# Layer 2's residual in the third stage: from vector additions to accumulating transfers, and from a written-out order to a table of phases

## The chip, the cores and the metric

The kernel runs on one core of one Trainium2 chip. The metric is the device time of one execution in microseconds (us), as the median of three runs. A core has a matrix engine (TensorE, PE in the profile, with PEld for its weight loads), a vector engine (VectorE, DVE), a scalar engine (ScalarE, ACT), GpSimd (POOL) and SyncE (SP), which here only issues transfers. Each engine takes its own instructions strictly in order and waits for the others through semaphores.

## The reference

A batch of 8192 images of 8 channels, 16 by 16, goes through four residual layers. Each layer adds a convolution-like map of the group-normalised input to that input:

```python
x = x + L0(gn(x))      # a tensor-train product over channel, row and column, plus a bias
x = x + L1(gn(x))      # 3x3 convolution, batch normalisation over the whole batch, relu
x = x + L2(gn(x))      # 3x3 convolution of values quantised to -127..127, plus a bias per channel
x = x + L3(gn(x))      # 3x3 convolution with binarised weights, edge padding, plus a bias per channel
```

`gn` subtracts the mean and divides by the standard deviation over 4 groups of 2 channels. Layer 2's quantisation needs the largest absolute value of the whole normalised batch, and layer 1 needs its batch statistics; so the kernel has three stages, each of which goes through all data once.

## The kernel before

The batch is cut into NT = 64 tiles of 128 images. A tile is a 128 x 2048 float32 array: channel and row on the 128 partitions, image and column on the free axis. The first stage computes layer 0 and layer 1's convolution, the second stage the rest of layer 1 and the maximum for layer 2, the third stage (lines 880 to 1053) layers 2 and 3 of every tile. The change touches the third stage alone.

In the third stage the steps of tile i are functions, one instruction or a few each:

- `rows2` (L907, VectorE, two small instructions), `spread2` (L917, TensorE): layer 2's scale per image, spread over the partitions into PSUM.
- `scale2`, called `v` (L925, VectorE, two instructions of 1024 columns): x times the scale, rounded to 8 bits. `round2`, called `q` (L933, ScalarE): to bfloat16.
- `layer2` (L942, TensorE): the convolution of half a tile, h = 0 or 1, six matmuls into a PSUM tile `pq` of two banks. In the order these are `c2h0` and `c2h1`.
- The residual of layer 2. Half 0: `bias2` (L938, ScalarE) adds the bias to x in place, and `first2`, called `stz` (L951, VectorE), adds the scaled PSUM tile to x. Half 1: `second2`, called `z1` (L955, ScalarE), evacuates the PSUM tile with scale and bias into the scratch `z3[i % 2]`, and `add2`, called `add1` (L958, GpSimd), adds it to x.
- `square3` (`sq`, L962, ScalarE), `sums3` (`sums`, L965, TensorE: 16 matmuls onto 32 columns), `stats3` (`small`, L969, VectorE: five small instructions), `pow3` (L973, GpSimd), `rows3` (L910, VectorE), `spread3` (L920, TensorE): the statistics of layer 3's normalisation.
- `offset3` (`c`, L976, ScalarE), `scale3` (`t`, L982, VectorE, two instructions), `high3` (`hi`, L993, ScalarE, with the edge columns), `low3` (`lo`, L998, GpSimd), `edges3` (`edl`, L1011, ScalarE), `add3` (`corr`, L1003, GpSimd: adds offset and bias to x). For the last three tiles `offset3` does nothing and `add3` runs on VectorE.
- `layer3` (L1014, TensorE): half a tile, 24 matmuls in all for both halves, first those of `hi`, then those of `lo`, into a PSUM tile `pf` of two banks (`c3h0`, `c3h1`). `finish` (`out0`, `out1`, L1025, VectorE) adds it to x, and the second of the two sends the tile out.

The PSUM tiles `pq` and `pf` share one tag, `pc`, with two buffers (L882): they are given out in turn, in the order in which the program asks for them, so each new one waits until the tile two before it has been read.

The order of the stage is a list of (step, tile) pairs. Every engine keeps the order of the list (`InOrder`, L33). The list is `C_HEAD`, written out by hand, then a repeated `TURN` (L1040), then `C_TAIL`, written out by hand. At each `rows2:i` the tile i + 4 is also loaded.

```python
        TURN = [("rows2", 3), ("rows3", -1), ("out1", -3), ("sq", 0), ("c2h0", 1), ("stz", 1), ("spread2", 3), ("spread3", -1),
                ("c", -1), ("c2h1", 1), ("z1", 1), ("add1", 1), ("v", 3), ("sums", 0), ("small", 0), ("pow", 0), ("t", -1),
                ("edl", -2), ("q", 2), ("hi", -1), ("bias", 2), ("lo", -1), ("corr", -1), ("c3h0", -2), ("out0", -2),
                ("c3h1", -2)]
```

Of the kernel before, what the change touches and what calls it, by code (L numbers as in the profile page):

```python
# [8 lines left out]
F32 = mybir.dt.float32  # L9
# [3 lines left out]
AF = mybir.ActivationFunctionType  # L13
ALU = mybir.AluOpType
# [4 lines left out]
P = 128  # L19
C, H, W = 8, 16, 16  # L20
# [5 lines left out]
QS = P // NQ  # L26
BANK = QS * W
# [17 lines left out]

C_HEAD = """
rows2:0 spread2:0 v:0 rows2:1 q:0 spread2:1 c2h1:0 rows2:2 bias:0 v:1 spread2:2 rows2:3 c2h0:0 v:2 z1:0 q:1
spread2:3 stz:0 add1:0 bias:1 c2h1:1 sq:0 c2h0:1 z1:1 v:3 sums:0 stz:1 small:0 q:2 add1:1 c2h0:2 c2h1:2 bias:2  # L50
rows2:4 pow:0 sq:1 rows2:5 rows3:0 z1:2 spread2:4 spread3:0 stz:2 t:0 q:3 sums:1 hi:0 c:0 small:1 v:4 add1:2 pow:1
bias:3 c2h0:3 spread2:5 rows3:1 sq:2 c2h1:3 spread3:1 stz:3 lo:0 sums:2 t:1 rows2:6 corr:0 edl:0 small:2 c:1 q:4
z1:3 hi:1 c3h0:0 pow:2 c3h1:0 v:5 add1:3 rows3:2 out0:0 bias:4 out1:0 lo:1 sq:3 q:5 spread3:2 spread2:6 c2h0:4 c:2
corr:1 edl:1 c2h1:4 rows2:7 z1:4 stz:4 t:2 hi:2 sums:3 c3h1:1 small:3 v:6 c3h0:1 out1:1 c2h1:5 pow:3 bias:5 rows3:3
spread3:3 lo:2 out0:1 q:6 spread2:7 rows2:8 z1:5 edl:2 v:7 c:3 add1:4 sq:4 c2h0:5 c3h0:2 bias:6 t:3 corr:2 stz:5
sums:4 c3h1:2 small:4 add1:5 hi:3 out0:2 c2h0:6 pow:4 rows3:4 sq:5 out1:2 spread2:8 stz:6 spread3:4 t:4 lo:3 c2h1:6
z1:6 corr:3 edl:3 sums:5 c:4 hi:4 small:5 pow:5 bias:7 v:8 q:7 add1:6
""".split()
C_TAIL = """
c2h1:-4 sq:-5 rows2:-2 rows3:-6 out1:-8 spread3:-6 rows2:-1 spread2:-2 c2h0:-4 v:-2 sums:-5 stz:-4 z1:-4 q:-3 t:-6  # L60
edl:-7 c3h0:-7 q:-2 small:-5 c2h1:-3 c:-6 out0:-7 c2h0:-2 hi:-6 add1:-4 sq:-4 pow:-5 rows3:-5 z1:-3 spread3:-5
bias:-2 t:-5 stz:-2 lo:-6 edl:-6 sums:-4 small:-4 bias:-3 corr:-6 c:-5 spread2:-1 c2h0:-3 stz:-3 pow:-4 c3h1:-7
hi:-5 out1:-7 c3h0:-6 rows3:-4 spread3:-4 add1:-3 c2h1:-2 sq:-3 lo:-5 z1:-2 out0:-6 v:-1 c3h1:-6 edl:-5 q:-1 add1:-2
sums:-3 t:-4 corr:-5 c:-4 c3h1:-5 out1:-6 small:-3 sq:-2 pow:-3 hi:-4 out1:-5 lo:-4 rows3:-3 bias:-1 sums:-2 c2h1:-1
small:-2 z1:-1 spread3:-3 edl:-4 c2h0:-1 c3h0:-5 c:-3 t:-3 stz:-1 add1:-1 pow:-2 corr:-3 rows3:-2 c3h1:-4 hi:-3
spread3:-2 sq:-1 out0:-5 c:-2 corr:-4 sums:-1 t:-2 lo:-3 hi:-2 small:-1 pow:-1 out1:-4 c3h0:-4 corr:-2 rows3:-1
out0:-4 edl:-3 c3h0:-3 spread3:-1 t:-1 lo:-2 c3h1:-3 out0:-3 edl:-2 out1:-3 hi:-1 c:-1 lo:-1 c3h0:-2 c3h1:-2 edl:-1
out0:-2 c3h0:-1 out1:-2 corr:-1 c3h1:-1 out0:-1 out1:-1
""".split()

# [6 lines left out]
def tile_net(ctx: ExitStack, tc: tile.TileContext, xb, xt_in, pack0, pack1, pack2, out):  # L79
    nc = tc.nc  # L80
    NT = xt_in.shape[0]

    pe, dve, act, pool = (InOrder(tc, e) for e in (nc.tensor, nc.vector, nc.scalar, nc.gpsimd))
# [78 lines left out]
    L = {}  # L162
# [127 lines left out]
    HALVES = [(0, P // 2), (P // 2, P)]  # L290

    def samples(t):
        return t.rearrange("p (b w) -> p b w", w=W)

    def over_w(stat, a, b):

        return stat[:, a:b].unsqueeze(2).to_broadcast([P, b - a, W])
# [25 lines left out]
    with first as s:  # L323
        small = s.enter_context(tc.tile_pool(name="small1", bufs=3))
# [5 lines left out]
        T = [dict() for _ in range(NT)]  # L330
# [267 lines left out]
        for n in range(NT * NQ):  # L598
            t, q = divmod(n, NQ)
# [62 lines left out]
        t = NT - 1  # L662
# [84 lines left out]
    small = ctx.enter_context(tc.tile_pool(name="small", bufs=4))  # L747
    kept = {}
    with tc.tile_pool(name="p2", bufs=2) as p2, tc.tile_pool(name="ps2", bufs=2, space=PSUM) as ps2:
        T = T2  # L750
# [8 lines left out]
        for k in range(3):  # L759
            nc.tensor.matmul(kps, L["gpad"].rearrange("p q j -> p (q j)"), L["band3"][:, k],  # L760
                             start=(k == 0), stop=(k == 2))
# [83 lines left out]
        for i in range(NT + 4):  # L845
# [4 lines left out]
            elif late:  # L850
                k, j = late.pop(0)
# [12 lines left out]
    inv = const.tile([P, 1], F32, name="inv")  # L864
# [15 lines left out]
    with ExitStack() as s:  # L880
        wk = s.enter_context(tc.tile_pool(name="wk3", bufs=2))
        ps_c = s.enter_context(tc.tile_pool(name="ps_c3", bufs=2, space=PSUM))  # L882
# [4 lines left out]
        T = [dict() for _ in range(NT)]  # L887
# [16 lines left out]
        def halves(t):  # L904
            return t.rearrange("p (h n) -> p h n", h=2)
# [29 lines left out]
            act.copy(q, T[i].pop("v"))  # L935
            T[i]["q"] = q

        def bias2(i):  # L938
            x = halves(T[i]["x"])[:, 0]
            act.activation(x, x, AF.Identity, bias=L["bias2"], scale=1.0)  # L940

        def layer2(i, h):  # L942
            pc = ps_c.tile([P, 2, BANK], F32, name=f"pq_{i}_{h}", tag="pc")
            for k in range(2):
                pv, xv = samples(pc[:, k]), samples(T[i]["q"])[:, (2 * h + k) * QS:(2 * h + k + 1) * QS]
                pe.matmul(pv, L["band2"][:, 1], xv, start=True, stop=False)
                pe.matmul(pv[:, :, 1:W], L["band2"][:, 0], xv[:, :, 0:W - 1], start=False, stop=False)
                pe.matmul(pv[:, :, 0:W - 1], L["band2"][:, 2], xv[:, :, 1:W], start=False, stop=True)
            T[i]["pq", h] = pc.rearrange("p k n -> p (k n)")

        def first2(i):  # L951
            x = halves(T[i]["x"])[:, 0]
            dve.scalar_tensor_tensor(x, T[i].pop(("pq", 0)), inv, x, ALU.mult, ALU.add)

        def second2(i):  # L955
            act.activation(z3[i % 2], T[i].pop(("pq", 1)), AF.Identity, bias=L["bias2"], scale=inv)

        def add2(i):  # L958
            x = halves(T[i]["x"])[:, 1]
            pool.tensor_tensor(x, x, z3[i % 2], ALU.add)  # L960

        def square3(i):  # L962
            act.activation(sq3, T[i]["x"], AF.Square)
# [10 lines left out]
            stats_pow(T[i]["mv"])  # L974

        def offset3(i):  # L976
            if i >= NT - 3:
                return
            T[i]["c"] = small.tile([P, P], F32, name=f"c_{i}", tag="c")
            act.activation(T[i]["c"], o3, AF.Identity, bias=L["bias3"], scale=1.0)  # L980

# [20 lines left out]

        def add3(i):  # L1003
            x = samples(T[i]["x"])
            if i >= NT - 3:
                for a, b in HALVES:
                    dve.scalar_tensor_tensor(x[:, a:b], over_w(o3, a, b), L["bias3"], x[:, a:b], ALU.add, ALU.add)
                return
            pool.tensor_tensor(x, x, over_w(T[i].pop("c"), 0, P), ALU.add)

        def edges3(i):  # L1011
            edges(T[i]["lo"])

        def layer3(i, h):  # L1014
            pc = ps_c.tile([P, 2, BANK], F32, name=f"pf_{i}_{h}", tag="pc")
            for m, t in enumerate(("hi", "lo")):
                for k in range(2):
                    q = 2 * h + k
                    tv = T[i][t][:, q * QS:(q + 1) * QS]
                    for n in range(3):  # L1020
                        pe.matmul(samples(pc[:, k]), L["sign3"][:, n], tv[:, :, n:n + W],
                                  start=(m == n == 0), stop=(m == 1 and n == 2))
            T[i]["pf", h] = pc

        def finish(i, h):  # L1025
            x = halves(T[i]["x"])[:, h]
            pc = T[i].pop(("pf", h)).rearrange("p k n -> p (k n)")
            dve.scalar_tensor_tensor(x, pc, L["scale3"], x, ALU.mult, ALU.add)
            T[i]["done"] = T[i].get("done", 0) + 1
            if T[i]["done"] == 2:  # L1030
                nc.sync.dma_start(out[order[i]], T[i]["x"])
                T[i].clear()

        OPS = {"rows2": rows2, "spread2": spread2, "v": scale2, "q": round2, "bias": bias2,
               "c2h0": lambda i: layer2(i, 0), "stz": first2, "c2h1": lambda i: layer2(i, 1), "z1": second2, "add1": add2,
               "sq": square3, "sums": sums3, "small": stats3, "pow": pow3, "rows3": rows3, "spread3": spread3, "c": offset3,
               "t": scale3, "hi": high3, "lo": low3, "corr": add3, "edl": edges3,
               "c3h0": lambda i: layer3(i, 0), "out0": lambda i: finish(i, 0),
               "c3h1": lambda i: layer3(i, 1), "out1": lambda i: finish(i, 1)}
        TURN = [("rows2", 3), ("rows3", -1), ("out1", -3), ("sq", 0), ("c2h0", 1), ("stz", 1), ("spread2", 3), ("spread3", -1),  # L1040
                ("c", -1), ("c2h1", 1), ("z1", 1), ("add1", 1), ("v", 3), ("sums", 0), ("small", 0), ("pow", 0), ("t", -1),
                ("edl", -2), ("q", 2), ("hi", -1), ("bias", 2), ("lo", -1), ("corr", -1), ("c3h0", -2), ("out0", -2),
                ("c3h1", -2)]
        todo = [(op, i + k) for i in range(-3, NT + 4) for op, k in TURN if 0 <= i + k < NT]
        if len(todo) >= len(C_HEAD) + len(C_TAIL):
            head, tail = ([(op, int(i) + n) for op, i in (c.split(":") for c in l)] for l, n in ((C_HEAD, 0), (C_TAIL, NT)))
            todo = head + todo[len(head):len(todo) - len(tail)] + tail
        for i in range(AHEAD):
            load3(i)
        for op, i in todo:  # L1050
# [72 lines left out]
```

## Time and profile before

| what | value |
|---|---|
| time, median of 3 runs | 3834.26 us (3833.98 to 3834.51) |
| span of the profiled execution | 3831.5 us; what lies around the span in that execution is not given |
| third stage: first `rows2` to the end of the span | 3064.6 to 3831.5 us |
| one tile in the middle of the third stage (start of one `pq` group to the same of the next tile) | 11.55 us |
| ScalarE, one of each: q, z1, bias, sq, c, hi, edges of hi, edl | 1.90, 1.21, 1.15, 1.90, 0.35, 1.93, 0.55, 0.54 us |
| VectorE, one of each: v (both halves), t (both), stz, out | 2.35, 2.34, 1.28, 1.26 us |
| GpSimd, one of each: pow, lo, corr, add1 | 1.02, 4.27, 3.69, 2.42 us |

The page of the profile gives busy time, share of the span and the number of instructions of each engine. A row of windows gives the same for a stretch of time, with the granted clock of TensorE and the busy share of the transfer engines. A timeline line is: start in us from the span's start, length in us, engine, line, operation, what it writes <- what it reads, how many in a row, and in brackets how long the engine stood idle before it and for whom. The line of nearly all instructions is L43, the helper that records them, so they are told apart by their tiles: `pq` layer 2 in PSUM, `pf` layer 3 in PSUM, `s` the sums, `bs` in the third stage mostly the scratch `z3`, `q`, `v`, `sq`, `hi`, `lo`, `mv` as above, `xs`, `u`, `xk`, `ys` (and `bs`) the places where x lies, `sq` and `xh` also the places of `t`.

### The profile page before, as it was taken

To read this page: it belongs to the slowest core of one execution; us is meant where nothing else is said; L and a number is where in the kernel's file an instruction comes from. 1 tells how busy PE (TensorE), PEld (TensorE's weight loads), DVE (VectorE), ACT (ScalarE), POOL (GpSimd) and SP (SyncE) were. 2 spreads that over 40 slices of the span, in tenths; PEclk is the share of its full clock that TensorE was granted. 3 is DMA by queue.
4 is the path that set the end of the run, shared out by engine and by line. 5 is a ranking of instruction groups with operands and counts; after the bars stand their busy time and mean duration, and the time that the engine had idled before them with its cause. 6 is when DMAs were issued, how large, how long until landed. Compare 5 with 4: busy or idle time off the path is not lost. (4 is left out here: it accounts for less than half of the span.)

```text
span 3831.5 us, 52833 instructions
## 1 busy us (share of the span) xinstructions
PE 3606.5 (94%) x16326; PEld 2127.6 (56%) x16326; DVE 3406.9 (89%) x6319; ACT 2513.1 (66%) x2673; POOL 3040.9 (79%) x3101
## 2 busy tenths in 40 slices
PE   8999999999999999999999999997655599999998
PEld 4666666666666666666666666662211155555555
DVE  8988888888888888888888888877998889999997
ACT  5666666666666666666666666665665477777775
POOL 4877778777777787777777877766887779999997
PEclk9999999999999999999999999998776699999999
DMA  5787787888877878788788788757999724444432
GB/s 212 255 268 258 258 266 251 270 253 262 270 256 258 267 250 271 253 262 267 258 261 266 250 271 252 258 187 281 422 425 425 301 110 176 187 185 178 185 145 99
DMA packets 210809, 960.93 MB, mean 251 GB/s; under 512 B 44896, under 2 KB 45152, under 8 KB 110048
## 3 DMA queue, kind: packets, MB, share of 16 engines
q1 hardware_dynamic: 173808, 692.22, 48.7%
q0 software_dynamic: 36288, 264.26, 23.4%
q8 instruction: 131, 2.15, 0.2%
q14 instruction: 150, 1.23, 0.1%
q10 hardware_dynamic: 432, 1.08, 0.1%
HBM read 578.84 MB, written 378.54 MB: 250 GB/s over the span
## 5 line engine op out<-in xcount | busy, mean ns | idle before, releaser
L43 PE MATMUL po<-u,core 128*128 128x512 f32 (+1 forms) x4112 | 1844.7, 591 | 0.0
L43 ACT COPY u<-pu 128x2048 f32<-128x2048 f32 x512 | 956.7, 1868 | 511.9 <-PE pu L43 511.8
L43 PEld LDWEIGHTS po<-u,core 128*128 128x128 f32 x4112 | 744.7, 190 | 737.1 <-issue 736.1
L43 PE MATMUL pu<-core2r,xl 128*128 128x256 f32 x4032 | 678.5, 310 | 4.5 <-ACT u L43 3.6
L43 PEld LDWEIGHTS pu<-core2r,xl 128*128 128x128 f32 x4032 | 527.9, 189 | 127.8 <-issue 123.0
L43 POOL TENSOR_TENSOR bs<-bs,xh 128x512 fp32r<-128x512 f32 (+1 forms) x253 | 325.6, 1287 | 201.0 <-ACT xh L43 200.9
L43 POOL TENSOR_TENSOR v<-e 128x128 f32<-128x128 f32 x750 | 397.9, 542 | 0.0
L43 DVE TENSOR_TENSOR xs<-po,xs 128x512 f32<-128x512 f32 x256 | 177.0, 692 | 217.5 <-PE po L43 217.5
L43 ACT ACTIVATE m<-pm,b 128x128 f32<-128x128 f32 x250 | 92.0, 368 | 395.5 <-PE pm L43 395.5
L43 PEld LDWEIGHTS pm<-v,fast 128*128 128x128 f32 x2000 | 262.5, 191 | 119.7 <-issue 106.2
L43 POOL TENSOR_TENSOR e<-x1n,x 128x512 f32<-128x512 f32 x250 | 306.2, 1225 | 23.9 <-ACT x L43 16.4
L43 DVE TENSOR_TENSOR bs<-bs,stat 128x1024 f32<-128x1024 f32 x252 | 290.8, 1217 | 2.1
L43 POOL TENSOR_TENSOR xs<-xs,w 128x2048 f32<-128x2048 f32 x64 | 291.5, 4554 | 0.6 <-DMA xs<-in_xt 0.6
L43 PE MATMUL pm<-v,fast 128*128 128x128 f32 x2000 | 263.6, 275 | 0.0
L43 ACT ACTIVATE x<-x1n 128x512 f32<-128x512 f32 x500 | 247.1, 545 | 7.6 <-DVE x1n L43 7.6
L43 POOL TENSOR_TENSOR mv<-mv,mhalf 128x4 f32<-128x4 f32 x127 | 130.8, 1030 | 138.1 <-DVE mv L43 138.1
L43 PE MATMUL pf<-hi,sign 128*128 128x512 f32 x768 | 227.7, 434 | 0.5 <-DVE xs L43 0.5
L43 POOL DMA_DIRECT2D xl<-limb_d x252 | 150.0, 595 | 96.9 <-ACT x L43 29.1
L43 PE MATMUL pf<-lo,sign 128*128 128x512 f32 x768 | 219.4, 423 | 0.0
L43 POOL TENSOR_TENSOR v<-r 128x128 f32<-128x128 f32 x500 | 215.9, 448 | 0.0
L43 ACT ACTIVATE sq<-xs 128x2048 f32<-128x2048 f32 x103 | 196.8, 1911 | 4.7 <-POOL xs L43 4.6
L43 PE MATMUL gb<-rows_c,sel 128*128 128x128 f32 x128 | 40.3, 409 | 167.3 <-DVE rows_c L43 167.3
(310 smaller groups left out, 7202.4 us busy)
## 6 DMA issues: line engine op xcount, KB each, us to landing
xl<-limb_d POOLq DMA_DIRECT2D x252, 1024.0 KB, 7.4
x_d<-xs SPq DMA_DIRECT2D x76, 1024.0 KB, 8.4
xs<-in_xt SPq DMA_DIRECT2D x64, 1024.0 KB, 7.5
bs<-in_xb SPq DMA_DIRECT2D x63, 1024.0 KB, 5.7
limb_d<-xh SPq DMA_DIRECT2D x1008, 64.0 KB, 4.3
limb_d<-bs SPq DMA_DIRECT2D x1008, 64.0 KB, 5.2
y_d<-ys SPq DMA_DIRECT2D x60, 1024.0 KB, 8.0
u<-x_d SPq DMA_DIRECT2D x34, 1024.0 KB, 5.9
```

The source lines that it names most:

```text
L43: return self.tc.keep_in_program_order(op(*args, **kwargs))
```

## The change

Layer 2's residual: both halves are now evacuated by ScalarE with scale and bias into a scratch of their own (`z0`, `z1`), and each is added to x by a transfer from SBUF to SBUF with addition, which GpSimd issues (`acc0`, `acc1`). `bias`, `stz` and `add1` go. The three last tiles are no longer an exception in `offset3` and `add3`. `layer3` is split into its `hi` part (a) and its `lo` part (b), so that other steps can stand between them. The lists `C_HEAD`, `TURN` and `C_TAIL` go: each step has a phase, and the list is sorted by 11.25 times the tile's number plus the phase.

```diff
-C_HEAD = """
...
-C_TAIL = """
...
+PERIOD = 11.25
+PHASE = {"rows2": 0, "spread2": 0.01, "v": 0.1, "q": 1.2, "c2h1": 8.1, "z1": 11.1, "acc1": 13, "c2h0": 14.9, "z0": 19.7,
+         "acc0": 19.8, "sq": 25.4, "sums": 33.8, "small": 33.81, "pow": 33.9, "rows3": 33.91, "spread3": 39.7, "c": 42.4,
+         "t": 45, "hi": 45.2, "lo": 51.1, "edl": 54.2, "corr": 55.9, "c3h1a": 56.3, "c3h1b": 56.31, "c3h0a": 56.4,
+         "out1": 56.41, "c3h0b": 56.42, "out0": 56.43}
...
-        def bias2(i):
-            x = halves(T[i]["x"])[:, 0]
-            act.activation(x, x, AF.Identity, bias=L["bias2"], scale=1.0)
...
-        def first2(i):
-            x = halves(T[i]["x"])[:, 0]
-            dve.scalar_tensor_tensor(x, T[i].pop(("pq", 0)), inv, x, ALU.mult, ALU.add)
-
-        def second2(i):
-            act.activation(z3[i % 2], T[i].pop(("pq", 1)), AF.Identity, bias=L["bias2"], scale=inv)
-
-        def add2(i):
-            x = halves(T[i]["x"])[:, 1]
-            pool.tensor_tensor(x, x, z3[i % 2], ALU.add)
+        def evacuate2(i, h):
+            act.activation(z3[h], T[i].pop(("pq", h)), AF.Identity, bias=L["bias2"], scale=inv)
+
+        def add2(i, h):
+            x = halves(T[i]["x"])[:, h]
+            pool.dma_start(x, z3[h], accum_op=ALU.add)
...
         def offset3(i):
-            if i >= NT - 3:
-                return
...
         def add3(i):
             x = samples(T[i]["x"])
-            if i >= NT - 3:
-                for a, b in HALVES:
-                    dve.scalar_tensor_tensor(x[:, a:b], over_w(o3, a, b), L["bias3"], x[:, a:b], ALU.add, ALU.add)
-                return
             pool.tensor_tensor(x, x, over_w(T[i].pop("c"), 0, P), ALU.add)
...
-        def layer3(i, h):
-            pc = ps_c.tile([P, 2, BANK], F32, name=f"pf_{i}_{h}", tag="pc")
-            for m, t in enumerate(("hi", "lo")):
-                for k in range(2):
-                    q = 2 * h + k
-                    tv = T[i][t][:, q * QS:(q + 1) * QS]
-                    for n in range(3):
-                        pe.matmul(samples(pc[:, k]), L["sign3"][:, n], tv[:, :, n:n + W],
-                                  start=(m == n == 0), stop=(m == 1 and n == 2))
-            T[i]["pf", h] = pc
+        def layer3(i, h, m):
+            if m == 0:
+                T[i]["pf", h] = ps_c.tile([P, 2, BANK], F32, name=f"pf_{i}_{h}", tag="pc")
+            pc, t = T[i]["pf", h], T[i]["hi" if m == 0 else "lo"]
+            for k in range(2):
+                q = 2 * h + k
+                tv = t[:, q * QS:(q + 1) * QS]
+                for n in range(3):
+                    pe.matmul(samples(pc[:, k]), L["sign3"][:, n], tv[:, :, n:n + W],
+                              start=(m == n == 0), stop=(m == 1 and n == 2))
...
-        TURN = [("rows2", 3), ("rows3", -1), ("out1", -3), ("sq", 0), ("c2h0", 1), ("stz", 1), ("spread2", 3), ("spread3", -1),
...
-            todo = head + todo[len(head):len(todo) - len(tail)] + tail
+               "c3h0a": lambda i: layer3(i, 0, 0), "c3h0b": lambda i: layer3(i, 0, 1), "out0": lambda i: finish(i, 0),
+               "c3h1a": lambda i: layer3(i, 1, 0), "c3h1b": lambda i: layer3(i, 1, 1), "out1": lambda i: finish(i, 1)}
+        todo = [(op, i) for _, op, i in sorted((PERIOD * i + at, op, i) for op, at in PHASE.items() for i in range(NT))]
```

Sorted, the middle of the stage repeats one cycle for each tile. With n the tile whose layer 3 is computed, each engine gets, in this order:

- TensorE: spread2:n+5, c3h1a:n, sums:n+2, c3h1b:n, c3h0a:n, c3h0b:n, c2h0:n+4, spread3:n+2, c2h1:n+5
- VectorE: rows2:n+5, t:n+1, small:n+2, v:n+5, out1:n, rows3:n+2, out0:n
- ScalarE: hi:n+1 (before it), q:n+5, sq:n+3, z0:n+4, c:n+2, edl:n+1, z1:n+5, then hi:n+2
- GpSimd: pow:n+2, acc1:n+4, lo:n+1, acc0:n+4, corr:n+1, then pow:n+3

More of the change, by code (lines that the diff above doesn't have):

```diff
@@ L44, in __getattr__ @@
         return call
-C_HEAD = """
[L49 to L58, printed above, removed]
-C_TAIL = """
-c2h1:-4 sq:-5 rows2:-2 rows3:-6 out1:-8 spread3:-6 rows2:-1 spread2:-2 c2h0:-4 v:-2 sums:-5 stz:-4 z1:-4 q:-3 t:-6
@@ L61 @@
[L61 to L69, printed above, removed]
+PERIOD = 11.25
[3 more added lines that the diff above has]
+         "out1": 56.41, "c3h0b": 56.42, "out0": 56.43}
@@ L1032, in finish @@
                 T[i].clear()
-        OPS = {"rows2": rows2, "spread2": spread2, "v": scale2, "q": round2, "bias": bias2,
-               "c2h0": lambda i: layer2(i, 0), "stz": first2, "c2h1": lambda i: layer2(i, 1), "z1": second2, "add1": add2,
+        OPS = {"rows2": rows2, "spread2": spread2, "v": scale2, "q": round2,
+               "c2h0": lambda i: layer2(i, 0), "z0": lambda i: evacuate2(i, 0), "acc0": lambda i: add2(i, 0),
+               "c2h1": lambda i: layer2(i, 1), "z1": lambda i: evacuate2(i, 1), "acc1": lambda i: add2(i, 1),
                "sq": square3, "sums": sums3, "small": stats3, "pow": pow3, "rows3": rows3, "spread3": spread3, "c": offset3,
                "t": scale3, "hi": high3, "lo": low3, "corr": add3, "edl": edges3,
-               "c3h0": lambda i: layer3(i, 0), "out0": lambda i: finish(i, 0),
-               "c3h1": lambda i: layer3(i, 1), "out1": lambda i: finish(i, 1)}
-        TURN = [("rows2", 3), ("rows3", -1), ("out1", -3), ("sq", 0), ("c2h0", 1), ("stz", 1), ("spread2", 3), ("spread3", -1),
[L1041 to L1046, printed above, removed]
-            todo = head + todo[len(head):len(todo) - len(tail)] + tail
+               "c3h0a": lambda i: layer3(i, 0, 0), "c3h0b": lambda i: layer3(i, 0, 1), "out0": lambda i: finish(i, 0),
+               "c3h1a": lambda i: layer3(i, 1, 0), "c3h1b": lambda i: layer3(i, 1, 1), "out1": lambda i: finish(i, 1)}
+        todo = [(op, i) for _, op, i in sorted((PERIOD * i + at, op, i) for op, at in PHASE.items() for i in range(NT))]
         for i in range(AHEAD):
```

## The prediction

> **What bounds the kernel now.** I read, in this order: the page's busy shares, the chain of work that ended last, the windows of the third stage, then the timelines of one tile.
>
> ```profile
> 3696.67 1.85 PE s L43 x16
> 3698.53 6.42 PE pf L43 x24
> 3704.95 1.31 PE pq L43 x6
> ```
>
> The chain runs through TensorE from 3132 to 3751 us, in pieces like these: nothing else ends last. The windows agree (after the stretch: busy us and instructions of PE, PEld, DVE, ACT, POOL; granted clock, transfer share, GB/s):
>
> ```profile
> 3300.00:3400.00 100.00, 100.00 (x509) 57.94 (x508) 93.15 (x167) 79.40 (x72) 97.58 (x35) 1.00 0.47 180
> ```
>
> TensorE is never idle, GpSimd nearly never. A busy TensorE need not be at its peak, so I take its starts:
>
> ```profile
> 3312.20 1.47 PE L43 MATMUL pq<-q,band 128*128 128x512 bf16 x6
> 3313.51 0.39 PE L43 MATMUL ps_a<-rows_d,sel 128*128 128x128 f32 x2
> ...
> 3314.18 1.46 PE L43 MATMUL pq<-q,band 128*128 128x512 bf16 x6
> 3315.57 1.06 PE L43 MATMUL s<-xs,wsum 128*32 128x512 f32 x8
> ...
> 3317.42 1.82 PE L43 MATMUL pf<-hi,sign 128*128 128x512 f32 x6
> 3319.08 1.71 PE L43 MATMUL pf<-lo,sign 128*128 128x512 f32 x6
> 3320.63 1.73 PE L43 MATMUL pf<-hi,sign 128*128 128x512 f32 x6
> 3322.19 1.71 PE L43 MATMUL pf<-lo,sign 128*128 128x512 f32 x6
> 3323.74 1.47 PE L43 MATMUL pq<-q,band 128*128 128x512 bf16 x6
> ```
>
> From start to start: pq 1.31, three spreads 0.67, pq 1.39 ahead of s, s 1.85, pf 1.66 behind s, then 1.55, 1.56, 1.55. That is 11.54 us a tile, the same to 0.01 us in every tile, and a group has these lengths wherever it stands (a pf group ahead of s takes 1.64, at 3781 us). So it is the cost of the matmuls and not of a wait: **no order of the same matmuls makes a tile shorter than 11.5 us**. The other engines:
>
> ```profile
> 3306.01 0.69 DVE L43 TENSOR_REDUCE s_d<-s 128x32 f32<-128x512 f32 x1 [0.23 <-PE s L43]
> ...
> 3307.47 2.34 DVE L43 TENSOR_TENSOR xh<-xs,ps_r 128x1024 f32<-128x1024 f32 x2
> 3308.24 2.42 POOL L43 TENSOR_TENSOR xs<-xs,bs 128x1024 f32<-128x1024 f32 x1
> 3309.73 1.28 DVE L43 SCALAR_TENSOR_TENSOR bs<-pf,scale,bs 128x1024 f32<-128x1024 f32 x1
> 3309.85 1.93 ACT L43 CAST hi<-xh 128x2048 fp32r<-128x2048 f32 x1 [2.28 <-DVE xh L43]
> ...
> 3313.31 1.89 ACT L43 ACTIVATE sq<-xs 128x2048 f32<-128x2048 f32 x1
> ...
> 3315.11 0.34 ACT L43 ACTIVATE c<-ps_o,bias 128x128 f32<-128x128 f32 x1
> 3315.67 1.21 ACT L43 ACTIVATE bs<-pq,bias,inv 128x1024 f32<-128x1024 f32 x1 [0.22 <-PE pq L43]
> ```
>
> They give the latencies used below: s_d starts 0.14 after the group behind s (3305.87); small is 1.46 (to 3307.47); ScalarE starts 0.04 after VectorE's end (3309.81); an engine's next instruction starts about 0.1 before the last one's end (sq 1.89, next at 1.80).
>
> [...] at the stage's start six pq matmuls take 2.51 us (3070.48), later 1.31. [...] No accumulating transfer is in this trace. [...] lo takes 4.27 us beside whatever VectorE runs.
>
> **The change, part by part.**
>
> Removed: bias (64 x 1.15 us of ScalarE), stz (64 x 1.28 of VectorE), add1 (64 x 2.42 = 155 of GpSimd). TensorE's 11.54 covered all three, so by themselves they are worth nothing.
>
> Added: z0, 64 x 1.21 on ScalarE, and two transfers a tile. *Issue on GpSimd*: the nearest row is the limb fetch, 595 ns[...]; I take 0.7. GpSimd then has 1.02 + 4.27 + 3.69 + 1.4 = 10.4 us a tile, with gaps 10.6. *Landing*: [...] 7.4 us (the limb fetch, 1 MB beside a 0.8 busy transfer side); I take 5. Share of the transfer engines: 0.47 x 11.55 = 5.4 us a tile for 2 MB now; 1 MB of accumulation adds 2.7[...], no bound. Neither bound can be a gain, since TensorE waits for neither now.
>
> Moved: everything, by the table. Call S the moment at which sums:n+2 ends on TensorE. From S the table gives TensorE c3h1b:n, c3h0a, c3h0b, c2h0:n+4, spread3, c2h1:n+5, spread2, c3h1a:n+1, sums:n+3. Its groups, with the lengths above: 1.66 + 1.56 + 1.55 + 1.31 + 0.45 + 1.31 + 0.22 + 1.64 + 1.85 = 11.55, no gain. But VectorE now has **v:n+5 behind small:n+2**, ScalarE has q:n+5, sq:n+3, z0:n+4 in a row, and the two PSUM buffers alternate, so c3h1a:n+1 takes the one that z0:n+4 has to empty. That closes a ring of one tile:
>
> S, 0.14, small 1.46, v 2.34, 0.04, q 1.80, sq 1.80, z0 1.21, 0.10 to TensorE (0.05 from q to pq at 3070.48; VectorE's 0.15 at most), c3h1a 1.64, sums 1.85 = **12.38 us**.
>
> A second ring goes S, 0.14, small 1.46, v 2.26, out1 1.19, rows3 0.79, out0 1.26, 0.15, c2h1 1.31, spread2 0.22, c3h1a 1.64, sums 1.85 = 12.27 (c2h1 takes out0's buffer, c2h0 out1's). Both exceed TensorE's 11.55, so the period is 12.38: 0.83 us a tile. TensorE stands 0.5 us ahead of c2h0, 0.2 ahead of c2h1, 0.1 ahead of c3h1a[...].
>
> Waits beside the ring: acc0:n+4 waits on GpSimd for z0's end (S + 8.8); behind it are corr:n+1 (to S + 13.2) and pow:n+3, whose input comes at S + 14.0; covered as long as an issue takes under 1.5 us. lo:n+1 ends at S + 7.7, before edl on ScalarE (S + 9.0). sq:n+3 starts at S + 5.8 and its transfer was issued at S - 3.5: 9.3 us for a landing of 5. Loads and stores on SP keep their places at rows2 and out; a load's slot was sent out four tiles before.
>
> The head, from rows2:0 (3064.6) as 0: v:0 to 3.8, q:0 5.8. c2h1:0 stands ahead of spread2:1 and runs at half clock, to 8.4; v:1 to 11.3, q:1 13.2, c2h1:1 15.4, v:2 18.2, q:2 20.1, c2h1:2 22.0, sums:0 24.2, small:0 25.8. From here the ring binds, without c3: v:3 28.1, q:3 30.1, sq:1 31.9, sums:1 33.8, small:1 35.4, v:4 37.8, q:4 39.7, sq:2 41.5, z0:3 42.6, c3h1a:0 44.4, sums:2 **46.2**. Landings up to 6.5 us hide behind q.
>
> 59 periods follow, while there are tiles for v: 59 x 12.38 = 730.4.
>
> The tail, from the end of sums:61, at 11.55 or less: sums:62 10.0, sums:63 18.7, c3 of 61 23.5, spread3:63 23.9, c3h1a:62 25.5; lo:62 follows pow:63 on GpSimd, so c3h1b:62 starts at 26.3, c3 of 62 ends at 31.0. Now that corr is on GpSimd to the end, corr:62 (3.7) stands ahead of lo:63, to 33.7; edl 34.3, c3 of 63 39.0, out0 40.4, and 5.0 for the last store as now (its issue follows 3826.4): **45.4**.
>
> Sum: 46.2 + 730.4 + 45.4 = 822.0 against 3831.5 - 3064.6 = 766.9: +55.1 (59 x 0.83 = 49, head and tail 6). The profiled execution's span becomes 3886.6; the runs' median lies 2.8 above the span, which I keep: **3889 us**.
>
> **The rivals.** *TensorE stays dense* (the other side): if c3h1a does not wait for z0, nor c2h1 for out0, because buffers go to whichever tile frees one first, both rings are open and the period is 11.55: 46.2 + 681.5 + 45.4 = 773.1, +6, 3840 us: no change, or with a shorter head a small gain. It decides once the rings fall below 11.55. For it: the alternation is read in the code, not seen. Against it: with two buffers the next to come free is z0's anyway.
> *Late landings*: at over 9.3 us from issue to landing sq waits for acc0 and the period grows by the excess; at 10.5 us 13.6, +71, 3960 us. For it: 19.6 us landings under a full transfer side in the second stage. Against it: this stage uses 0.47.
> *GpSimd as the bound*: 9.2 + 2 issues exceeds 12.38 from 1.6 us an issue; at 2.0 13.2, +48, 3938 us.
>
> **How the numbers follow.** Chances: forecast 0.72, dense 0.06, a gain at head and tail on top of that 0.02, late landings 0.12, GpSimd 0.08. The forecast's own range is 3889 +- 16 (0.15 us of latencies x 59 = 9, head and tail 7). To hold 8 in 10 the range takes in GpSimd's case and the first of the late landings: 3868 to 3942. A measurement of this kernel can tell about 0.2% (8 us) from no change. Faster 0.02, same 0.06, slower 0.92.
>
> **What would show it.** Right: starts of s_d 12.4 us apart; TensorE's share near 93% in the stage, its idle time ended by VectorE (ahead of pq) and ScalarE's bs (ahead of pf); ScalarE idle about 3 us ahead of each q for v; no wait for a transfer ahead of sq. Wrong: s_d 11.55 apart (dense), sq waiting for a transfer, or pow waiting behind an issue of 1.6 us and more.

## The result, and the profile after

The changed kernel takes 3898.74 us (3897.29 to 3900.11), the kernel before beside it 3834.12: a ratio of 1.0171, interval 1.0159 to 1.0184. It is **slower by 64.6 us**; 3889 was forecast, 3868 to 3942 the range. The profiled execution has 3898.44 us and a span of 3896.7, so 1.7 us lie around the span.

The windows of the stage (after the stretch: busy us and instructions of PE, PEld, DVE, ACT, POOL; granted clock, transfer share, GB/s):

```profile
3400.00:3500.00 100.00, 96.96 (x459) 55.38 (x465) 74.98 (x144) 72.20 (x66) 87.09 (x41) 1.00 0.89 254
```

Every engine's busy share fell against the row shown of before, and 459 matmuls stand in 100 us where 509 stood in that row (from 3300 to 3700 us, 1841 for 2016): no engine is full any more. The transfer engines went from 0.47 to 0.89.

The timeline of one cycle of the changed kernel, which is where the prediction's rings can be read off:

```profile
3402.55 0.69 DVE L43 TENSOR_REDUCE s_d<-s 128x32 f32<-128x512 f32 x1 [2.82 <-PE s L43]
3404.01 2.35 DVE L43 TENSOR_TENSOR v<-xk,ps_a 128x1024 int8<-128x1024 f32 x2
3405.61 1.72 PE L43 MATMUL pf<-lo,sign 128*128 128x512 f32 x6
3406.39 1.90 ACT L43 CAST q<-v 128x2048 bf16<-128x2048 int8 x1 [3.44 <-DVE v L43]
3407.61 1.46 PE L43 MATMUL pq<-q,band 128*128 128x512 bf16 x5 [0.28 <-DVE u L43]
3408.20 1.91 ACT L43 ACTIVATE sq<-u 128x2048 f32<-128x2048 f32 x1
3409.56 1.47 PE L43 MATMUL pq<-q,band 128*128 128x512 bf16 x6
3410.01 1.19 ACT L43 ACTIVATE bs<-pq,bias,inv 128x1024 f32<-128x1024 f32 x1
3410.86 0.39 PE L43 MATMUL ps_a<-rows_d,sel 128*128 128x128 f32 x2
3411.25 1.81 PE L43 MATMUL pf<-hi,sign 128*128 128x512 f32 x6
3412.99 1.06 PE L43 MATMUL s<-u,wsum 128*32 128x512 f32 x8
3414.98 0.69 DVE L43 TENSOR_REDUCE s_d<-s 128x32 f32<-128x512 f32 x1 [2.82 <-PE s L43]
```

From s_d to s_d 12.43 us, the same to 0.03 in all 59 cycles. A ring is a chain of waits that comes back to the same step one tile later, so the sum of its pieces is the period. Follow it here: s_d to v 1.46, v to q 2.38, q to sq 1.81, sq to z0 (the first `bs`) 1.81, z0 to c3h1a 1.24, c3h1a to s 1.74, s to s_d 1.99: 12.43. TensorE's own loss is 0.44 us ahead of c2h0 (start to start 2.00, where 1.56 is the group's length), 0.22 ahead of c2h1 (ps_o starts at 3409.12, and 0.22 is its length) and 0.25 ahead of c3h1a (0.39 behind ps_a, where 0.14 is enough): 0.91, and 12.43 - 0.91 = 11.52 us of matmuls. sq starts straight behind q: no transfer holds it up.

The longest wait of the stage in the changed kernel (us in total, times, longest; 3300 to 3700 us) is ScalarE's ahead of q, the 3.4 us of the timeline, once a tile:

```profile
ACT q L43 <- DVE v L43: 110.3, 32, 3.5
```

The account of the span, 65.2 us more: 59 cycles of 12.434 us in place of 11.546 make 52.4; the rest, 12.8, is head and tail.

### The profile page after: what moved, and what is told of

The parts are those of the page before. It is cut to its first block, busy times and chain, and to the rows that moved or that the text cites. A ratio compares the mean times of both kernels' runs of the same rounds, so it can differ in the third digit from the quotient of the medians.

```text
span 3896.7 us, 52947 instructions
## 1 busy us (share of the span) xinstructions
PE 3644.1 (94%) x16264; PEld 2137.3 (55%) x16326; DVE 3312.4 (85%) x6249; ACT 2510.6 (64%) x2676; POOL 3021.3 (78%) x3168
## 3 DMA queue, kind: packets, MB, share of 16 engines
q14 instruction: 152, 1.24, 0.1%
## 4 chain that ended last, share of the span: by engine, by line
PE 75%; DVE 17%; issue 3%; DMA 3%; POOL 1%; ACT 1%; POOLq 0%; DVEq 0%; SPq 0%; ACTq 0%
PE po L43 44%; PE pu L43 12%; PE pm L43 6%; PE pf L43 3%; PE s L43 3%; DVE top L43 3%; PE pc L43 3%; DVE v L43 3%; PE pq L43 3%; DVE xs L43 2%; DVE u L43 2%; DVE s_d L43 1%; DVE ys L43 1%; DVE xk L43 1%; PE gb L43 1%
## 5 line engine op out<-in xcount | busy, mean ns | idle before, releaser
L43 POOL TENSOR_TENSOR e<-x1n,x 128x512 f32<-128x512 f32 x250 | 306.2, 1225 | 21.8 <-ACT x L43 14.3
L43 ACT CAST q<-v 128x2048 bf16<-128x2048 int8 x64 | 121.5, 1899 | 230.8 <-DVE v L43 214.2
L43 PE MATMUL pq<-q,band 128*128 128x480 bf16 (+1 forms) x706 | 190.7, 391 | 31.6 <-ACT q L43 9.1
```

Source lines behind the costliest of these rows:

```text
L43: return self.tc.keep_in_program_order(op(*args, **kwargs))
```

## The experiments

**Theory**: small ahead of v on VectorE ties each tile's start to the last one's sums; two rings of nearly equal length follow, through ScalarE (q, sq, z0) and through VectorE (out1, rows3, out0). **Rivals**: the new residual is itself the cost (landing of the transfers, GpSimd's issues, ScalarE's second evacuation); or the order on ScalarE alone.

### v ahead of small

```diff
-PHASE = {"rows2": 0, "spread2": 0.01, "v": 0.1,
+PHASE = {"rows2": 0, "spread2": 0.01, "v": 0.03,
```

> One phase of the changed kernel is altered: v gets 0.03 in place of 0.1, so VectorE runs v:n+5 ahead of small:n+2 and no longer behind it. Ring theory: this takes small out of the way of v, q, sq, z0 and c3h1a, and v out of the way of out1, rows3, out0 and c2h1 (that ring falls from 12.27 to about 10.0 us), so TensorE is dense again: starts of s_d 11.55 to 11.65 us apart in place of 12.43, 59 x 0.85 = 50 us less, about 3845 us (3838 to 3855). Theory that the transfers bind (their engines are 0.89 busy at 12.43 us a tile, 11.1 us of work): the spacing stays at 12.2 or more, 3885 us or more, with sq waiting for acc0. Theory that GpSimd binds: the spacing stays as well, with GpSimd never idle.

Measured: 3845.02 us, ratio to the kernel before 1.0030 (1.0019 to 1.0041). s_d is 11.53 us apart. The window of this kernel:

```profile
3400.00:3500.00 100.00, 99.58 (x496) 58.36 (x503) 82.48 (x158) 80.17 (x69) 92.93 (x45) 1.00 0.96 273
```

496 matmuls, with the accumulating transfers in place and the transfer engines at 0.96. One swap of two neighbours on one engine gives back 53.7 of the 64.6 us (52.3, if each kernel is set against the kernel before that was timed beside it): small ahead of v was the cost, and the rest is head and tail. The transfer engines now stand close behind TensorE: 0.96 of 11.53 us is 11.1 us a tile.

### Without the transfers

Layer 2's result is not added to x in this kernel; everything else is as in the kernel after.

```diff
-"acc1": 13, ... "acc0": 19.8, 
```

> The changed kernel without its accumulating transfers: both halves are still evacuated, but layer 2's result is not added to x, so that part of the computation is left out. Ring theory: no transfer is in the ring, the spacing of s_d stays at 12.4 us; the head is about 4 us shorter, because GpSimd's first addition[...] no longer stands behind two issues: 3894 us (3888 to 3898). Theory that the transfers or their issues are the cause: the spacing falls towards 11.55, about 3845 us.

Measured: 3894.61 us, ratio 1.0163 (1.0146 to 1.0180), s_d 12.43 apart. The same wait, in this kernel:

```profile
ACT q L43 <- DVE v L43: 110.3, 32, 3.5
```

Unchanged: the transfers lie in no ring of this order. Most of the 4.1 us by which this kernel is faster is in the head: the third s_d comes at 3112.72 us for 3116.63. What the transfers take can be read by difference: the transfer engines fall from 0.89 to 0.44, and from pow's start to lo's end GpSimd takes 5.27 us in place of 6.21 (with one issue between), so an issue costs it 0.94 us, 0.65 ahead of lo and 0.28 by which lo's record is longer.

### sq ahead of q

```diff
-"sq": 25.4,
+"sq": 23.5,
```

> The kernel after with sq:n+3 ahead of q:n+5 on ScalarE (its phase 23.5 in place of 25.4), in the time in which ScalarE is idle ahead of q. Theory (two rings of nearly the same length, each closed by small being ahead of v on VectorE): the ring through q, sq and z0 loses sq's 1.8 us and falls to about 10.6, but the ring through out1, rows3, out0, c2h1 and c3h1a is untouched and binds at 12.3 us, so almost nothing is won: s_d 12.3 us apart, some 7 us in all, about 3891 us (3885 to 3898). Rival (the order q, sq, z0 on ScalarE alone is the cost, and VectorE's part in the second ring is covered): 1.8 us less a tile, to TensorE's 11.55, about 3847 us. Second rival (sq now stands ahead of its accumulating transfer's landing, issued 3.5 us before the end of the sums): sq waits for the transfer, q behind it starts later, 3900 us or more.

Measured: 3883.68 us, ratio 1.0133 (1.0120 to 1.0147): 15 us less, where 7 were expected, and just outside the expected 3885 to 3898. s_d is 12.17 apart. The timeline shows the second ring alone:

```profile
3408.24 0.69 DVE L43 TENSOR_REDUCE s_d<-s 128x32 f32<-128x512 f32 x1 [2.57 <-PE s L43]
3409.70 2.35 DVE L43 TENSOR_TENSOR v<-ys,ps_a 128x1024 int8<-128x1024 f32 x2
3410.48 1.92 ACT L43 ACTIVATE sq<-xk 128x2048 f32<-128x2048 f32 x1 [2.27 <-DMA xk<-bs]
3411.97 1.28 DVE L43 SCALAR_TENSOR_TENSOR u<-pf,scale,u 128x1024 f32<-128x1024 f32 x1
3413.95 1.24 DVE L43 SCALAR_TENSOR_TENSOR u<-pf,scale,u 128x1024 f32<-128x1024 f32 x1
3415.25 1.47 PE L43 MATMUL pq<-q,band 128*128 128x512 bf16 x6
3416.70 1.79 PE L43 MATMUL pf<-hi,sign 128*128 128x512 f32 x6
3420.41 0.69 DVE L43 TENSOR_REDUCE s_d<-s 128x32 f32<-128x512 f32 x1 [2.56 <-PE s L43]
```

1.46 to v, 2.27 to out1, 1.98 to out0, 1.30 to c2h1, 1.31 to spread2 (3416.56), 0.14 to c3h1a, 1.72 to s (3418.42), 1.99 to s_d: 12.17. So taking 1.8 us out of the one ring wins 0.26, because the second was right behind it; TensorE's 11.52 stay out of reach as long as small is ahead of v. The rival that put the cost on ScalarE's order alone (3847) falls. sq now does wait for its transfer, up to 3.4 us, but in time in which ScalarE was idle anyway.

### The order of before with the new residual

```diff
+        new = {"bias": [], "stz": ["z0", "acc0"], "add1": ["acc1"]}
+        todo = [(o, i) for op, i in todo for o in new.get(op, [op])]
```

> The kernel before, its order kept (written-out head and tail, repeated turn, VectorE's addition for the last three tiles), with layer 2's residual done as in the change: bias drops out, stz becomes z0 and acc0, add1 becomes acc1. Ring theory: the order is the cause, so TensorE stays dense at 11.55 us a tile and the time is near that of before, 3825 to 3845 us; GpSimd has room, but acc1 now stands behind corr and lands late for sq, so a few tenths a tile may be lost. Theory that the transfers are the cause: 12.2 us a tile or more, 3880 us or more.

Measured: 3994.16 us, ratio 1.0424 (1.0407 to 1.0442): **the theory that the order alone is the cause missed**, by some 150 us. The time lies where the other one, that the transfers are the cause, had put it (3880 us or more); for this order it is right. ScalarE and GpSimd in its timeline:

```profile
3407.11 1.91 ACT L43 ACTIVATE sq<-xs 128x2048 f32<-128x2048 f32 x1 [4.26 <-DMA xs<-bs]
3408.93 1.19 ACT L43 ACTIVATE bs<-pq,bias,inv 128x1024 f32<-128x1024 f32 x1
3410.27 1.20 ACT L43 ACTIVATE bs<-pq,bias,inv 128x1024 f32<-128x1024 f32 x1
...
3411.77 0.88 POOL L43 DMA_DIRECT2D u<-bs  x1 [0.44 <-ACT bs L43]
...
3420.31 1.91 ACT L43 ACTIVATE sq<-u 128x2048 f32<-128x2048 f32 x1 [3.76 <-PE pq L43]
```

In that list sq:n stands ahead of z0:n+1 and z1:n+1, and acc1 follows z1. That is a ring through the landing: sq to z0 1.82, to z1 1.34, to the issue 1.50, to the next sq 8.54: 13.20 us, the distance of the two sq. I had looked for rings through the engines and had not carried the landing round. This kernel has no fixed period: between head and end of the stage two sq are 10.5 to 23.1 us apart, 13.9 on average, so 13.2 is what the ring took in this cycle. From 3300 to 3700 us sq waits for a transfer in 27 of 29 tiles. Why the distances vary so much stays open. The wait ahead of the second sq is put down to TensorE's pq, which sq neither reads nor writes, so I took the transfer to have ended it as it did a cycle earlier; the next experiment takes the transfers out.

### The order of before, new residual, no transfers

Layer 2's result is not added here either.

```diff
-        new = {"bias": [], "stz": ["z0", "acc0"], "add1": ["acc1"]}
+        new = {"bias": [], "stz": ["z0"], "add1": []}
```

> The order of the kernel before with both halves of layer 2 evacuated by ScalarE and the accumulating transfers left out (layer 2's result is not added). It tells what made the old order with the new residual 13.2 us a tile. Theory (a ring through the landing: sq:n, z0:n+1, c, z1:n+1, issue of acc1:n+1, landing 8.5 us, sq:n+1; 1.8 + 1.1 + 0.25 + 1.2 + 0.3 + 8.5 = 13.2): without transfers the ring is open and TensorE's 11.55 us return, 3836 us (3830 to 3846). Rival (the second evacuation on ScalarE, between sq and z1, is the cost by itself): the period stays above 12.5 us, 3900 us or more.

Measured: 3832.19 us, ratio 0.9997 (0.9989 to 1.0006), s_d 11.55 apart. The transfers were the whole 162 us (their issues went with them; by the waits of sq, it was the landing), and the second evacuation on ScalarE costs nothing here. It says more: with the addition gone altogether, the kernel is no faster than before. In this order, in which TensorE fills the stage with its matmuls, no form of the residual can be worth anything.

### The table's order with the old residual, twice

The steps bias, stz, z1 and add1 are those of the kernel before again: first with bias ahead of c2h0 in the list (phase 14.8), then with bias at phase 11.3, which is earlier and not one period later, as the expectation has it: straight behind z1, ahead of hi, q and sq:

```diff
-"z0": 19.7, "acc0": 19.8, "acc1": 13,
+"add1": 13, "bias": 14.8, "stz": 19.7,
```

```diff
-"bias": 14.8,
+"bias": 11.3,
```

> The changed kernel with its table of phases and the split of layer 3, but with layer 2's residual as before: bias on ScalarE (phase 14.8), stz on VectorE at z0's phase, add1 on GpSimd at acc1's phase, no transfers between SBUF and SBUF. Ring theory: v, behind small, still holds up out1, rows3, out0 and with it c2h1; the ring through z0 is gone, but that through out0 stays: 12.27 us a tile, so 59 x 0.15 = 9 us less than the changed kernel, and 4 us less at the head [...]: 3885 us (3875 to 3895). Theory that the transfers are the cause: 11.55 us a tile, about 3840 us.

> The order of the table with the residual of the kernel before (bias, stz, add1), as in the experiment of the old residual, but with bias one period later, behind z1 and ahead of hi on ScalarE (phase 11.3 in place of 14.8), where ScalarE is idle. Theory (there, bias behind q and sq held up stz, which held up rows2, spread2 and c3h1a): stz now follows out0 at once on VectorE, and the ring is 0.14, small 1.46, v 2.26, out1 1.19, rows3 0.8, out0 1.2, stz 1.2, rows2 0.5, 0.25, spread2 0.25, c3h1a 1.73, sums 1.85 = 12.8 us a tile: about 3920 us (3900 to 3935). Rival (bias is not what made stz late): above 4000 us. Second rival (once bias is out of the way the old residual has the same ring as the new one): 12.2 us, 3885 us.

Measured: 4053.0 us, ratio 1.0575 (1.0559 to 1.0591), s_d 14.3 or 15.9 us apart, 14.9 on average, where both theories had less than 3900 us; then 3903.13 us, 1.0181 (1.0166 to 1.0197). The timeline of the first shows why it missed:

```profile
3414.50 1.91 ACT L43 ACTIVATE sq<-xs 128x2048 f32<-128x2048 f32 x1
3416.32 1.13 ACT L43 ACTIVATE u<-u,bias 128x1024 f32<-128x1024 f32 x1
...
3417.48 1.28 DVE L43 SCALAR_TENSOR_TENSOR u<-pq,inv,u 128x1024 f32<-128x1024 f32 x1 [1.67 <-ACT u L43]
...
3419.24 0.49 PE L43 MATMUL ps_a<-rows_d,sel 128*128 128x128 f32 x2 [1.91 <-DVE rows_d L43]
```

bias stood behind q and sq, stz waited for bias, rows2 stands behind stz on VectorE, and spread2 with c3h1a and the sums behind rows2: one more ring, with a wait that my edit had added. Out of the way (11.3), the period is 12.57, with stz (1.2) in the second ring; the sum gave 12.8, and the time lies within the expected 3900 to 3935. So in the table's order the new residual's ring (12.43) is 0.14 us a tile shorter than the old one's: the residual is not what makes this order slow.

### GpSimd's pause in the head

The head of the changed kernel took 52.0 us (3064.5 to the end of sums:2), 46.2 were predicted. GpSimd's timeline there, kernel after:

```profile
3063.24 0.38 POOL L851 PARTITION_ALL_REDUCE gm<-pm  x1 [8.51 <-DVE pm L850]
...
3087.84 0.85 POOL L43 DMA_DIRECT2D xk<-bs  x1 [5.58 <-ACT bs L43]
3095.73 1.05 POOL L43 TENSOR_TENSOR mv<-mv,mhalf 128x4 f32<-128x4 f32 x1 [7.04 <-issue]
```

pow:0 starts 7.0 us behind an issue and waits for nothing that is shown; its input was there at 3091.5. The trace has two MODIFY_POOL_CONFIG instructions right behind that issue (3088.5), and in the kernel before, where an addition comes next on GpSimd, right behind the all-reduce (3063.7). So I took the 7.0 us to come with the first arithmetic instruction behind the all-reduce, and not with the issues. Edit, with a result that nothing uses (the expectations further down call it "the early library"):

```diff
     nc.gpsimd.partition_all_reduce(gm, pm, P, bass_isa.ReduceOp.max)
+    pool.tensor_tensor(pm, pm, mhalf[:, 0:1], ALU.mult)
```

> The kernel after with one small GpSimd multiplication right behind the all-reduce ahead of the third stage (its result is used by nothing). Theory (in the head pow:0 starts 4.2 us late [...]): [...] pow:0 starts right behind mv at about 3091.5, and the head is 4.2 us shorter: 3894.5 us (3893 to 3897), the period 12.43 as before. Rival (the 7 us ahead of pow:0 are the cost of the four issues that stand in front of it[...]): pow:0 stays where it is, 3898.7 us.

Measured: 3895.34 us, ratio 1.0164 (1.0150 to 1.0178). That interval overlaps that of the kernel after, so the reading rests on the trace of this kernel:

```profile
3070.68 0.18 POOL L43 TENSOR_TENSOR pm<-pm,mhalf 128x1 f32<-128x1 f32 x1 [7.02 <-issue]
...
3092.00 1.06 POOL L43 TENSOR_TENSOR mv<-mv,mhalf 128x4 f32<-128x4 f32 x1 [2.69 <-DVE mv L43]
```

The 7 us moved to where nobody waits, pow:0 now waits for VectorE alone, and the third s_d comes 3.3 us earlier (3113.35 for 3116.63), the period as before. The rival (the issues themselves) falls.

### Order edits together, and confined

```diff
+    pool.tensor_tensor(pm, pm, mhalf[:, 0:1], ALU.mult)
-PHASE = {"rows2": 0, "spread2": 0.01, "v": 0.1,
+PHASE = {"rows2": -3.2, "spread2": -3.19, "v": 0.03,
...
+            if i >= NT - 3: (offset3 and add3 as in the kernel before)
```

> The kernel after with four edits of the order around its residual: v ahead of small (the ring opened, 11.52 us a tile), the early library, rows2 and spread2 of a tile ahead of c2h1 of the tile before it (phases -3.2 and -3.19), and corr of the last three tiles on VectorE again. Theory: 3845.0 of the kernel with v first, less 4.2 for the library, 2.5 for the two waits for lo at the end, and about 3 for spread2:1 ahead of c2h1:0 in the head: 3835 us (3832 to 3841), no faster than the kernel before, since TensorE's 11.5 us a tile set the stage in both. Rival (the new residual or its order costs something else that the ring had covered): above 3843 us. Second rival (the new residual is worth something once TensorE is dense): below 3828 us.

Measured: 3855.79 us, ratio 1.0059 (1.0047 to 1.0072): a miss by 21, and worse than v ahead of small alone. The head was 6.8 us shorter (third s_d at 3107.99 for 3114.79), but the period rose to 11.83: spread2, now ahead of c2h1, waits in every tile for rows2. On TensorE ps_o starts at 3409.96, spread2 at 3410.39 and c2h1 at 3410.72: 0.43 and 0.33, where 0.22 each is the length. The 0.31 us by which the period is above 11.52 make 18 us in 59 tiles, and the end was 2.0 longer (30.8 us from the last s on, for 28.8), which I put down to corr on VectorE ahead of t. Then each edit only where it helps:

```diff
+        def early(op, i, at):
+            if i < 4 and op in ("rows2", "spread2"):
+                return at - 3.2
+            return 56.35 if i >= NT - 2 and op == "corr" else at
```

(corr of the last two tiles on VectorE; v at 0.03 and the added multiplication kept)

> The kernel after with v ahead of small, the early library, rows2 and spread2 moved ahead (by 3.2) for the first four tiles alone, and corr on VectorE, behind t, for the last two tiles alone. Theory: the combined kernel's head was 6.8 us shorter than that of the kernel with v first (end of sums:2 at 3108.0 and 3114.8), but its spread2 waited for rows2 in every tile, 0.31 us each, and corr on VectorE ahead of t made its end 1.9 us longer; with both confined the sum is 3845.0 - 6.8 - 1.4 (the wait for lo of the last tile) = 3837 us (3833 to 3841), period 11.53. Rival (the head is won only because tiles further on start early, and is given back behind it): 3843 to 3846 us.

Measured: 3835.03 us, ratio 1.0006 (0.9998 to 1.0014), period 11.53: the time of the kernel before, with the new residual in place. The end is 27.9 us from the last s on. The window of this kernel:

```profile
3400.00:3500.00 100.00, 99.53 (x500) 58.01 (x507) 83.06 (x152) 78.34 (x70) 93.65 (x43) 1.00 0.96 272
```

So with the transfers in place nothing of the loss is left: it was order and place, and not the cost of the new addition. No version that does the whole computation beat the kernel before.

## Why the prediction was right

**Floor and period.** TensorE's 11.55 us as the floor: 11.52 as the sum of the groups in the changed kernel, 11.53 measured in two orders (v ahead of small, edits confined). "The same in every tile" holds for the kernel before in its middle, some 53 tiles; nearer the ends its s_d are 5 to 18 us apart. Ring through ScalarE 12.38: 12.43 measured, every term within 0.1. Second ring 12.27: 12.17, with 0.11 less from out0 to c2h1, 0.08 less for spread2 ahead of c3h1a (0.14 for 0.22) and 0.08 more from c3h1a to s. Stalls 0.5, 0.2 and 0.1 ahead of c2h0, c2h1, c3h1a: 0.44, 0.22, 0.25. The 59 periods: 730.4 predicted, 733.6 measured. That the mechanism is this one is shown by v ahead of small, which opens both rings.

**The head, the term that was mis-sized most**: 46.2 against 52.0. The end of sums:0 was 1 us late, and 4.7 came between sums:0 and sums:1. I had looked at what bias, stz and add1 cost and found them free; what add1 did beside its work, being GpSimd's first arithmetic behind the all-reduce, was not on my list (in the kernel before add1:0 waits 10.84 us for bs there, and pow:0 has no pause ahead of it). The added multiplication gives back 3.3 us; what is left, some 2.5, I did not take apart (the granted clock is 0.73 over the head, 0.50 from 3064 to 3075 us as in the kernel before, and six groups of pq there take 1.96 to 2.77 us, where I counted one so and a record at granted clock 1.00 is 1.47).

**The tail**: 45.4 against 46.6. TensorE waits for lo in each of the last two tiles: c3h1b starts 3.22 and 3.15 us behind c3h1a, where 1.64 and 1.55 are enough, so 1.6 us each. The prediction's times hold 0.8 and 1.8. The first is the one that was too short: pow:63 stands behind corr:61 for some 0.6 us, and lo's record there is 4.67 us and not 4.27.

**Around the span**: 2.8 us taken, 1.7 measured. This 1.1 us goes the other way from the errors of head (5.8), periods (3.2) and tail (1.2).

**What surrounds the ring.** *Issue*: 0.7 taken, my estimate above the 595 ns of the limb fetch, 0.94 measured, below the 1.5 at which corr would have held up pow; GpSimd takes 10.8 us a tile (87.1% of 12.43) for my 10.4. *Landing*: 5 taken, my estimate below the 7.4 of the limb fetch with its 1 MB, 5.0 the median, against a slack of 9.3. *Transfer engines*: 0.89 x 12.43 = 11.1 us a tile, of which the accumulation is 0.45 x 12.43 = 5.6 for 1 MB, and the plain 2 MB 5.5. So a byte of the accumulation took twice the time of a plain one. From 3300 to 3700 us the accumulations move 33.76 MB in 9264 packets and the plain transfers 67.51 MB in 9280: their packets are half as long as well, so a price per packet would show the same, and no run separates the two.

**The rivals.** *Dense*: wrong, the buffers do alternate (c3h1a starts 0.05 us behind z0's end, at 3411.20). *Late landings*: not in this order, but that kind of ring, at 13.9 us on average, is what the old order has with the new residual; my 9.3 us of slack came from the table, not from the transfer. *GpSimd as the bound*: no.

**The signs.** s_d 12.4 apart, ScalarE idle 3.4 ahead of q, idle time of TensorE ended by VectorE ahead of pq and by bs ahead of pf, no transfer ahead of sq: all seen. TensorE's share in the window was a bad sign: 97% for my 93%, although it does lose 0.91 of 12.43 us. A group's record goes on beyond the start of the next (pq 1.46 us long, 1.30 apart; the ends of matmuls are modelled in this profile), so the share hides short stalls; starts and the count of matmuls (1841 for 2016 in 400 us) show them.

## What to carry to other kernels

An order in which each engine looks dense can still close a ring from one tile to the next: write the steps of one cycle in a row, from the end of one reduction to the next, and compare the sum with the bound engine's floor; where two rings are close, mending one wins only their difference. Ask of every asynchronous step how far its landing is from its next use in that very order: the same transfers cost 4 us in one order and 162 us in another. And when an instruction is removed, look at what it started besides its own work.

## What the runs showed of the hardware

- An accumulating transfer of 512 KB from SBUF to SBUF took 0.94 us of GpSimd and a median of 5.0 us to landing at a transfer share of 0.89 (medians of 7.0 to 8.1, by the place of x, in the old order, where the two of a tile are issued about 1.4 us apart). 1 MB of it took 5.6 us of the transfer engines, where 1 MB of plain transfers in twice as long packets took 2.7.
- GpSimd's lo and corr, which follow an issue, have records of 4.55 and 4.00 us, 4.28 and 3.69 in the kernel without transfers. A longer record is not longer work: at the end of the changed kernel, with no issue between them, the records are longer still, and yet the next instruction starts as soon as in the kernel without transfers. There lo:61 (at 3863.18 us, the first lo behind the last issue) has a record of 4.71 us and corr one of 4.11, but they take 4.24 and 3.65 us from start to start, for 4.23 and 3.65 without transfers.
- Behind the all-reduce, GpSimd's pause of 7.0 us came ahead of the first arithmetic instruction that followed (7.04 us ahead of pow:0 in the changed kernel, 7.02 ahead of the multiplication added in front of it); the four transfer issues in between did not bring it on.
- VectorE, ScalarE and GpSimd started their instructions in the order of the list in every cycle of the changed kernel from 3300 to 3700 us. v, which stands behind small there, started 1.46 us behind s_d; ahead of small in the list, it no longer held the period at 12.43 us, which fell to 11.53.
